# Graph-layer maximum on one core: a shorter chunk part, one-hot columns on GpSimd between gathers, and x theta^T kept in HBM

## The chip, the core and the metric

One NeuronCore of a Trainium2 chip runs the whole kernel. The metric is device time in microseconds (us). Engines: TensorE (PE; PEld is its weight load), VectorE (DVE), ScalarE (ACT), GpSimd (POOL) and SyncE (SP), each with an instruction queue of its own. An indirect DMA (a "gather") fetches one row per partition from HBM by an index in SBUF; GpSimd issues it.

## The reference

`x` is 6250 x 256 float32; 100,000 edges come sorted by `dst`. The weights `theta_w` and `phi_w` are 256 x 256.

```python
x_src, x_dst = x[src], x[dst]
theta_x = (x_dst - x_src) @ theta_w.T + theta_b
phi_x = x_src @ phi_w.T + phi_b
e = relu(theta_x + phi_x)
out = segment_max(e, dst, num_segments=6250)
out = where(isfinite(out), out, 0.0)
return layernorm(x + out)          # eps 1e-5, no affine part
```

For an edge into node n the value is relu(A[n] + B[src]), with A = x theta^T and B = x (phi - theta)^T + both biases. A is the same for all edges of a node, so the kernel takes the maximum of B[src] over the edges of each node and adds A, the relu, x and the normalisation afterwards.

## The kernel before

**Two parts.** B is computed first and written to `b_rows` in HBM. The edges, in the order of `dst`, are then treated in two ways.

*The chunk part* takes the first 128 x `FIRST_STEPS` = 128 x 275 edges, which belong to the first nodes (2154 of them, N1). Each partition holds 275 consecutive edges. A step gathers `b_rows` for one edge of every partition (`gather`, L468); 8 steps are a group (`STEPS`, `gather_group`), so there are 35 groups. `run` (L717) takes a running maximum along a partition's edges on VectorE, which starts anew wherever the node changes (L722, one instruction of 256 columns a step), and writes the group to `maxima_1` in HBM. Segments that cross partitions are mended by `heads_1` (L829), a gather, a maximum and a scatter.

*The node part* has the other 4096 nodes, `TILES` = 32 to a partition (one block of 128 nodes is a tile). It looks up where each node's edges begin (`begin`, from a window of 640 edges by Sign on ACT, L628), gathers each node's source list (`gather_run`, L472, 32 table gathers, read at L475), and then fetches rows of B by matmul instead of by DMA. B's 6250 rows are cut into 17 slots of 375 (`KB` = 3 blocks of 125). For each slot, `choice` (L877, on VectorE, two slots at a time, so nine batches) picks for each node at most one edge whose source lies in it, and `wanted` (L912: transpose on TensorE, a cast `rows` on ACT) writes the row's number to `chosen_rows` in HBM. `slot_part(s, c)` (L939) does a slot for 1024 nodes (four chunks, `CHUNKS`, so 68 parts): it loads the chosen numbers into all partitions (`want`, L945), makes a one-hot matrix `hot` of 128 x 1024 for each of the three blocks, block 0 on VectorE (L949, is_equal) and blocks 1 and 2 on ACT (L951 Abs, L952 Relu), multiplies the slot's rows by it on TensorE in 24 matmuls of 512 columns (L959; each float32 row is split in two `terms` that add up to it), and keeps the maximum in `acc` on VectorE (L970; the first slot is copied by ACT). `slot_terms` (L926) loads a slot's rows and splits them.

Edges that a slot had no place for go into lists (`list_pieces`, L980): `LIST` = 240 steps, 30 groups, which `group_2` (L1044) gathers from `b_rows` and reduces as the chunk part does, into `maxima_2`.

**The order.** The program issues: the sort branch (not taken here: the edges come sorted), table gathers, B, `sources` (L853), nine times `choice`, `wanted` and two chunk groups, the heads of chunks, `list_pieces` with a part between, then the remaining chunk groups with 1.2 parts a group (`PACE`), then the list groups, again with 1.2 parts a group, every third of them with a share of the finishing of the first part's nodes (`rows_of`, L1051, and `normalise`, L1096), then the finish of the node part's 32 tiles. `rows_of` loads x, transposes it, multiplies by theta (L1077), gathers the maxima by node (L468 from `maxima_1` or `maxima_2`, 49 in all), and adds; `normalise` does the layer norm (ACT L1104, L1111). The framework's scheduler may move an instruction on its engine as its dependencies allow.

Gathered groups lie in a ring of 7 tiles (`gathered`, `RING`). Chunk groups 0, 2, 4, 6 and 8 (`X_GROUPS` = 5) gather x itself, before B is there, two of them ahead of the sort branch, and `b_of` (L663) turns the rows into B. B of the whole x goes through `b_of` two tiles at a time: four transposes, an ACT copy `x_t`, four matmuls of 256 columns (L675), and the bias on VectorE (L678).

Of the kernel before, what the change touches and what calls it, by code (L numbers as in the profile page):

```python
# [52 lines left out]
RING = 7  # L53
GENERAL_STEPS = 17
FIRST_STEPS = 275
X_GROUPS = 5
X_BEFORE = 2
TILES = 32
LIST = 240
WINDOW = 640  # L60
# [4 lines left out]
DVE_HOTS = 1  # L65
PACE = 1.2
# [339 lines left out]
def gnn_kernel(ctx: ExitStack, tc: tile.TileContext, x, src, dst, theta_w, theta_b, phi_w, phi_b, out):  # L406
# [4 lines left out]
    Q = N // P  # L411
    LEFT = N - P * Q
    NT = Q + 1
    XQ = 4
# [8 lines left out]
    NB = N // ROWS  # L423
    NS = -(-NB // KB)
# [4 lines left out]
    assert D == 2 * P and LEFT > 0 and LEFT1 > 0 and Q % XQ == 0 and OWN % CW == 0  # L429
    assert (P - 1) * T + 1 < E <= P * T and N < ID_MASK and P * T <= EDGES and E + 8 * P <= EDGES  # L430
    assert N == NB * ROWS and SLOT * NS < ABSENT and KB * P <= SLOT and WINDOW <= 8 * P and P * T1 < E
    assert LIST % STEPS == 0 and TILES <= 32

# [4 lines left out]

    b_rows = dram.tile([N, D], FP, name="b_rows")
# [5 lines left out]

    x_main = x[: P * Q, :].rearrange("(p q) d -> p q d", q=Q)
    b_main = b_rows[: P * Q, :].rearrange("(p q) d -> p q d", q=Q)
    b_block = b_rows.rearrange("(b r) d -> r b d", r=ROWS)


    x_1 = x[: P * Q1, :].rearrange("(p q) d -> p q d", q=Q1)
    x_2 = x[N1:, :].rearrange("(p q) d -> p q d", q=TILES)
    out_1 = out[: P * Q1, :].rearrange("(p q) d -> p q d", q=Q1)
    out_2 = out[N1:, :].rearrange("(p q) d -> p q d", q=TILES)
    maxima_1t = maxima_1[: P * T1, :].rearrange("(p t) d -> p t d", t=T1)
    maxima_2t = maxima_2[: P * LIST, :].rearrange("(p t) d -> p t d", t=LIST)

    def iota(t, step, base, per_partition):
        nc.gpsimd.iota(
            t,  # L460
            pattern=[[step, t.shape[1]]],
            base=base,
            channel_multiplier=per_partition,
            allow_small_or_imprecise_dtypes=True,
        )

    def gather(to, table, offsets):
        nc.gpsimd.indirect_dma_start(  # L468
            out=to, out_offset=None, in_=table, in_offset=bass.IndirectOffsetOnAxis(ap=offsets, axis=0)
        )  # L470

    def gather_run(to, table, offsets):  # L472

        n = to.shape[1]
        nc.gpsimd.indirect_dma_start(  # L475
            out=to,
            out_offset=None,
            in_=flat(table, 0, [[n, EDGES // n], [1, n]]),
            in_offset=bass.IndirectOffsetOnAxis(ap=offsets, axis=1),
        )  # L480
# [15 lines left out]

    for i in of_x[:X_BEFORE]:
        gather_group(i, x)
# [28 lines left out]

    weights = const.tile([P, 2, KC, D], FP, name="weights")
    bias = const.tile([P, 1, D], FP, name="bias")

# [13 lines left out]
    with (  # L544
# [4 lines left out]
        with tc.If(n_unsorted > 0):  # L549
# [4 lines left out]
            for i in of_x[:X_BEFORE]:  # L554
                gather_group(i, x)
# [51 lines left out]
    accs = body.enter_context(tc.tile_pool(name="accs", bufs=1))  # L607
    acc = accs.tile([P, KC, OWN], FP, name="acc")
    index = body.enter_context(tc.tile_pool(name="index", bufs=1))
    dst_w = index.tile([P, WINDOW], I32, name="dst_w")  # L610
    gather_run(dst_w, dst_list, edge0_i)
    for i in of_x[X_BEFORE:]:
        gather_group(i, x)
# [9 lines left out]
    BATCH = 8  # L623
    for j0 in range(0, TILES + 1, BATCH):
        j1 = min(j0 + BATCH, TILES + 1)
        for j in range(j0, j1):
            junk = index.tile([P, WINDOW], BF, name="junk")
            nc.scalar.activation(  # L628
                junk, local, AF.Sign, bias=halves[:, j : j + 1], scale=-1.0, accum_out=sums[:, j : j + 1]
            )  # L630
        nc.vector.tensor_scalar(begin[:, j0:j1], sums[:, j0:j1], 0.5, 0.5 * WINDOW, op0=ALU.mult, op1=ALU.add)
# [8 lines left out]

    with (
        tc.tile_pool(name="prep", bufs=1) as prep,
        tc.tile_pool(name="x_in", bufs=3) as x_in,
        tc.tile_pool(name="b_out", bufs=2) as b_out,
        tc.tile_pool(name="ps_t", bufs=3, space=PSUM) as ps_t,
        tc.tile_pool(name="ps_b", bufs=3, space=PSUM) as ps_b,
    ):
        w_in = prep.tile([P, 2, KC, D], FP, name="w_in")
        for i, w in enumerate((theta_w, phi_w)):
            nc.sync.dma_start(w_in[:, i], w.rearrange("(c p) k -> p c k", p=P))  # L650
        biases = prep.tile([P, 2, D], FP, name="biases")
        for i, b in enumerate((theta_b, phi_b)):
            nc.sync.dma_start(biases[:, i, :], flat(b, 0, [[0, P], [1, D]]))
        nc.vector.tensor_add(bias[:, 0, :], biases[:, 0, :], biases[:, 1, :])
        nc.vector.tensor_sub(w_in[:, 1], w_in[:, 1], w_in[:, 0])
        for i in (1, 0):
            for c in range(KC):
# [3 lines left out]
                nc.vector.tensor_copy(weights[:, i, :, c * P : (c + 1) * P], ps[:, 0])  # L661

        def b_of(to, rows):  # L663

            n = rows.shape[1]
            ps = ps_t.tile([P, 2, KC, P], FP, name="ps_xt")
            for i in range(n):
                for k in range(KC):
                    nc.tensor.transpose(ps[:, i, k, :], rows[:, i, k * P : (k + 1) * P], ident)
            x_t = prep.tile([P, 2, KC, P], FP, name="x_t", bufs=3)  # L670
            nc.scalar.copy(x_t[:, :n], ps[:, :n])  # L671
            ps = ps_b.tile([P, 2, D], FP, name="ps_b")
            for i in range(n):
                for k in range(KC):
                    nc.tensor.matmul(  # L675
# [474 lines left out]
    for j in todo:  # L1150
        node_place(j)
# [74 lines left out]
```

## Time and profile before

| what | value |
|---|---|
| median of 4 runs | 1128.27 us (1126.05 to 1139.71) |
| the profiled execution | 1127.52 us, its span 1125.7 |
| mean granted TensorE clock in the span | 0.783 of full speed |
| DMA over the span | 195.61 MB, 174 GB/s; HBM read 114.27 MB, written 81.38 MB |
| fetch matmuls, L959 | 1600, 432.6 us busy, mean 428 ns |
| chunk gathers, L468 from `b_rows` by `src` | 235, 277.5 us, mean 1181 ns |
| list gathers, L468 from `b_rows` by `list_src` | 240, 233.9 us, mean 974 ns |
| last gathers, L468 from `maxima` | 49, 48.5 us, mean 990 ns |
| running maximum, L722 | 513, 244.2 us, mean 478 ns |
| maximum into `acc`, L970 | 128, 155.5 us, mean 1215 ns |
| one-hot on ACT, L951 and L952 | 132 each, 146.1 and 133.9 us |
| matmuls of B, L675 | 356, 98.5 us |
| matmuls of A at the end, L1077 | 196 (128 for the node part, 68 for the first), 58.1 us |

Times are of one execution by the hardware profiler, engines are busy beside one another, and "idle before" names what ended an engine's idle time. A gather's row is GpSimd's time to issue it; the transfer is done by the DMA engines and lands later. B's last row is written at 139.4 us, the first chunk gather from `b_rows` is issued at 144.3, `choice` ends near 281, `list_pieces` near 338; the list groups run from 534 to 981, and the last write of `maxima` is issued at 1025.

### The profile page before, as it was taken

How to read it: one execution, taken by the hardware profiler on the slowest of the kernel's cores; microseconds unless marked ns; L12 is line 12 of the kernel's file. 1: busy time of each engine (PE TensorE's matmuls, PEld its weight loads, DVE VectorE, ACT ScalarE, POOL GpSimd, SP SyncE). 2: the span in 40 equal slices, each digit the busy share in tenths (PEclk: the TensorE clock that was granted, in tenths of full speed). 3: DMA queues.
4: the chain of work that ended last, by engine and by line, in shares of the span. 5: the costliest groups of instructions: out<-in, count | busy, mean ns of one | idle time of the engine just before them, and what ended most of it. 6: DMA issues, size and time to landing. Idle time of an engine off the chain costs nothing. (4 is left out here: it accounts for less than half of the span.)

```text
span 1125.7 us, 9291 instructions
## 1 busy us (share of the span) xinstructions
PE 644.4 (57%) x2557; PEld 499.0 (44%) x2557; DVE 630.3 (56%) x1309; ACT 429.8 (38%) x680; POOL 638.8 (57%) x622
## 2 busy tenths in 40 slices
PE   0475896485147451287659229447163976795473
PEld 0264784364035340165427128336152755674362
DVE  1221694799979731177487139345253775795264
ACT  0165121564114301166356036336232653650175
POOL 6745377588887777463706736737573657302600
PEclk9888898688658875597859659769585989899696
DMA  6455355477456753375648438546374656645322
GB/s 213 126 160 153 105 181 184 159 247 243 169 165 195 238 173 103 93 233 159 196 183 264 146 102 273 169 138 203 116 224 137 224 186 216 205 180 201 98 99 92
DMA packets 63082, 195.61 MB, mean 174 GB/s; under 512 B 14071, under 2 KB 22795, under 8 KB 53515
## 3 DMA queue, kind: packets, MB, share of 16 engines
q1 hardware_dynamic: 32207, 112.01, 28.3%
q0 software_dynamic: 28272, 75.14, 23.8%
q10 hardware_dynamic: 2540, 7.75, 1.8%
q8 instruction: 23, 0.38, 0.1%
q14 instruction: 40, 0.33, 0.1%
HBM read 114.27 MB, written 81.38 MB: 174 GB/s over the span
## 5 line engine op out<-in xcount | busy, mean ns | idle before, releaser
L959 PE MATMUL ps_f<-hot,terms 128*128 128x512 f32 x1600 | 432.6, 428 | 290.7 <-issue 107.2
L959 PEld LDWEIGHTS ps_f<-hot,terms 128*128 128x128 f32 x1600 | 327.9, 208 | 384.4 <-issue 217.9
L468 POOL DMA_INDIRECT g<-b_rows,src x235 | 277.5, 1181 | 109.3 <-issue 70.2
L468 POOL DMA_INDIRECT g<-b_rows,list_src x240 | 233.9, 974 | 160.8 <-issue 68.9
L970 DVE TENSOR_TENSOR acc<-acc,ps_f 128x1024 f32<-128x1024 f32 x128 | 155.5, 1215 | 249.5 <-remote 216.6
L951 ACT ACTIVATE hot<-want,minus_row 128x1024 fp32r<-128x1024 f16 x132 | 146.1, 1145 | 332.2 <-remote 218.0
L722 DVE SCALAR_TENSOR_TENSOR g<-g,caps 128x256 f32<-128x256 f32 x513 | 244.2, 478 | 21.5 <-issue 15.3
L952 ACT ACTIVATE hot<-hot 128x1024 fp32r<-128x1024 f32 x132 | 133.9, 1049 | 0.4
L675 PE MATMUL ps_b<-weights,x_t 128*128 128x256 f32 x356 | 98.5, 437 | 47.1 <-ACT x_t L671 32.8
L468 POOL DMA_INDIRECT g<-maxima,place x49 | 48.5, 990 | 105.5 <-issue 62.9
L675 PEld LDWEIGHTS ps_b<-weights,x_t 128*128 128x128 f32 x356 | 75.7, 219 | 66.4 <-ACT x_t L671 37.6
L1077 PE MATMUL ps_e<-weights,x_t 128*128 128x256 f32 x128 | 37.6, 442 | 34.2 <-ACT x_t L1073 18.2
L671 ACT COPY x_t<-ps_xt 128x512 f32<-128x512 f32 (+1 forms) x45 | 24.9, 578 | 76.7 <-remote 24.7
L949 DVE TENSOR_SCALAR hot<-want,row_id 128x1024 fp32r<-128x1024 f16 x68 | 51.0, 750 | 1.4 <-ACT hot L952 1.4
L475 POOL DMA_INDIRECT table_i<-src_list,begin_i x32 | 30.3, 946 | 33.4 <-DVE begin_i L632 24.5
L468 POOL DMA_INDIRECT g<-in_x_dram,src x40 | 39.1, 977 | 16.0 <-issue 11.3
L678 DVE TENSOR_TENSOR b_sb<-ps_b,bias 128x512 f32<-128x512 f32 (+1 forms) x25 | 16.6, 678 | 52.1 <-remote 23.0
L1077 PEld LDWEIGHTS ps_e<-weights,x_t 128*128 128x128 f32 x128 | 26.1, 215 | 42.2 <-ACT x_t L1073 22.5
L628 ACT ACTIVATE junk<-local,halves 128x640 bf16<-128x640 f32 x33 | 27.4, 829 | 31.5 <-DVE b_sb L678 17.8
L1077 PE MATMUL ps<-weights,x_t 128*128 128x256 f32 x68 | 20.5, 452 | 32.6 <-issue 18.4
L1104 ACT ACTIVATE squares<-g,r 128x256 bf16<-128x256 f32 x49 | 24.3, 498 | 33.9 <-DVE g L722 25.2
L1087 DVE TENSOR_TENSOR g<-g,ps_e 128x512 f32<-128x512 f32 (+1 forms) x17 | 11.1, 655 | 44.2 <-PE ps_e L1086 20.1
(194 smaller groups left out, 498.7 us busy)
## 6 DMA issues: line engine op xcount, KB each, us to landing
maxima<-g SPq DMA_DIRECT2D x64, 1024.0 KB
want<-chosen_rows SPq DMA_DIRECT2D x68, 256.0 KB
x_q<-in_x_dram SPq DMA_DIRECT2D x12, 512.0 KB
b_rows<-b_sb ACTq DMA_DIRECT2D x12, 512.0 KB
raw<-b_rows SPq DMA_DIRECT2D x16, 336.0 KB
g<-in_x_dram SPq DMA_DIRECT2D x5, 1024.0 KB
out_dram<-g SPq DMA_DIRECT2D x5, 1024.0 KB
g<-b_rows,list_src POOLq DMA_INDIRECT x240
```

The source lines that it names most:

```text
L468: nc.gpsimd.indirect_dma_start(out=to, out_offset=None, in_=table, in_offset=bass.IndirectOffsetOnAxis(ap=offsets, axis=0))
L475: nc.gpsimd.indirect_dma_start(out=to, out_offset=None, in_=flat(table, 0, [[n, EDGES // n], [1, n]]), in_offset=bass.IndirectOffsetOnAxis ...
L628: nc.scalar.activation(junk, local, AF.Sign, bias=halves[:, j : j + 1], scale=-1.0, accum_out=sums[:, j : j + 1])
L671: nc.scalar.copy(x_t[:, :n], ps[:, :n])
L675: nc.tensor.matmul(ps[:, i, :], x_t[:, i, k, :], weights[:, 1, k, :], start=(k == 0), stop=(k == KC - 1))
L722: nc.vector.scalar_tensor_tensor(g[:, k, :], last[part], caps[:, t : t + 1], g[:, k, :], op0=ALU.min, op1=ALU.max)
L949: nc.vector.tensor_scalar(hot[:, b, :], want, row_id[:, b : b + 1], None, op0=ALU.is_equal)
L951: nc.scalar.activation(hot[:, b, :], want, AF.Abs, bias=minus_row[:, b : b + 1], scale=1.0)
L952: nc.scalar.activation(hot[:, b, :], hot[:, b, :].bitcast(FP), AF.Relu, bias=1.0, scale=-1.0)
L959: nc.tensor.matmul(ps[:, w : w + 512], terms[:, part, b, h * P : (h + 1) * P], hot[:, b, w : w + 512], start=(i == 0), stop=(i == n - 1),)
L970: nc.vector.tensor_tensor(to, to, ps, op=ALU.max)
L1077: nc.tensor.matmul(a[:, i, :], x_t[:, 2 * i + c, :], weights[:, 0, c, :], start=(c == 0), stop=(c == KC - 1))
```

## The change

- **Sizes.** The chunk part has 146 steps a partition (19 groups, the last of two steps) instead of 275, the node part 40 nodes (5120 nodes; five chunks of 1024, so 85 parts), the lists 288 steps (36 groups), the window 800 edges.
- **One-hot of block 0 on GpSimd.** `slot_part` is split. `start_part` loads `want`, makes block 0's one-hot on GpSimd and blocks 1 and 2 on ACT; `finish_parts` issues the matmuls and the maxima. `gather_steps` calls `start_part` ahead of every fourth gather while its group has parts left: one part in a chunk group, two in a list group; `finish_parts` stands behind the group's `run`.
- **GpSimd's order is fixed.** `in_turn` gives each of these GpSimd instructions an order dependency on the one before, so that they run as the program is written. A gather that is neither followed by a one-hot nor has one to come in its group is followed by an iota of 144 columns into a scratch tile `pause`.
- **A = x theta^T beside B.** A pair of tiles is multiplied by both weights in matmuls of 512 columns; ACT copies A out and it is written to `a_rows` in HBM. `rows_of` loads it from there in place of transposes, copies and matmuls of its own.
- **Slots by consecutive rows.** A slot is 375 consecutive rows of B, row p*3+b in block b of partition p, so that a slot's load takes three whole rows a partition; `sources` computes the row's place accordingly.
- **Rings and small moves.** Three groups of x (one ahead of the branch) instead of five; a ring of 4 tiles for the chunk part, and one of 7 for the lists and the finish, which lies where the tables were. Of ten begin positions three are counted by Sign on ACT and seven by is_le with a sum on VectorE. `choice` is followed by one chunk group, not two. `heads_1` gathers after the fourth list group and scatters after the sixth. The finish takes shares of eight tiles, four a PSUM tile.

```diff
-RING = 7
...
-FIRST_STEPS = 275
-X_GROUPS = 5
-X_BEFORE = 2
-TILES = 32
-LIST = 240
-WINDOW = 640
+RING = 4
+RING_2 = 7
+FIRST_STEPS = 146
+X_GROUPS = 3
+TILES = 40
+LIST = 288
+WINDOW = 800
...
-DVE_HOTS = 1
-PACE = 1.2
+PAUSE = 144
...
+    pause = const.tile([P, PAUSE], FP, name="pause")
...
+    def in_turn(one):
+        if latest[0] is not None:
+            after = mybir.DependencyInfo(mybir.DependencyClass.NoSync, mybir.DependencyReason.DATA)
+            tc.add_manual_dep(one.ins, latest[0], after, reason="GpSimd's order")
+        latest[0] = one.ins.name
+    def indirect(out, in_, in_offset=None, out_offset=None):
+        in_turn(nc.gpsimd.indirect_dma_start(out=out, out_offset=out_offset, in_=in_, in_offset=in_offset))
+    def gather(to, table, offsets, alone=True):
+        indirect(to, table, bass.IndirectOffsetOnAxis(ap=offsets, axis=0))
+        if alone:
+            in_turn(iota(pause, 1, 0, 0))
...
+    def gather_steps(to, sources, n, starts):
+        for k in range(n):
+            more = False
+            if starts and (k + 1) % (STEPS // 2) == 0:
+                more = start_part()
+                starts = starts - 1 if more else 0
+            gather(to[:, k, :], b_rows, sources[:, k : k + 1], alone=not (more or starts))
...
+                x_t = x_transposed(x_q[:, i : i + w, :])
+                ps = ps_b.tile([P, 2, 2, D], FP, name="ps_b")
+                for h in range(w):
+                    for k in range(KC):
+                        nc.tensor.matmul(
+                            ps[:, h], x_t[:, h, k, :], weights[:, k], start=(k == 0), stop=(k == KC - 1)
+                        )
+                add_bias(b_sb[:, i : i + w, :], ps[:, :w, 0, :])
+                nc.scalar.copy(a_sb[:, i : i + w, :], ps[:, :w, 1, :])
+            nc.scalar.dma_start(node_rows(b_rows, *share), present(b_sb, *share))
+            nc.scalar.dma_start(node_rows(a_rows, *share), present(a_sb, *share))
...
-    def group_1(i):
-        if i not in of_x:
-            gather_group(i, b_rows)
+    def group_1(i, starts):
         t0, n = groups[i]
-        run(1, ring_tiles[i], n, caps_1, t0, maxima_1t)
+        if i in of_x:
+            g = ring_tiles[i]
+            for _ in range(starts):
+                start_part()
+        else:
+            g = gathered.tile([P, STEPS, D], FP, name="g")
+            gather_steps(g, src_1[:, t0 : t0 + n], n, starts)
+        run(1, g, n, caps_1, t0, maxima_1t)
+        finish_parts()
...
-        nc.gpsimd.indirect_dma_start(out=maxima_1, out_offset=at_heads, in_=heads, in_offset=None)
+        in_turn(iota(pause, 1, 0, 0))
+        yield
+        indirect(maxima_1, heads, out_offset=at_heads)
...
+        left = min(SLOT_ROWS, N - s * SLOT_ROWS)
+        whole = left // KB
+        even = whole // 16 * 16
+        for a, b in ((0, even), (even, whole)):
+            if b > a:
+                nc.sync.dma_start(
+                    raw[a:b], flat(b_rows, (s * SLOT_ROWS + a * KB) * D, [[KB * D, b - a], [D, KB], [1, D]])
+                )
...
+        nc.scalar.copy(terms[:, 0], raw)
+        nc.vector.tensor_tensor(terms[:, 1], raw, terms[:, 0].bitcast(FP), op=ALU.subtract)
...
+    parts = [(s, c) for s in range(NS) for c in range(CHUNKS)]
+    started = []
+    def start_part():
+        if not parts:
+            return False
+        s, c = parts.pop(0)
         if c == 0:
             slot_terms(s)
-        blocks = min(KB, NB - s * KB)
-        terms = terms_of[s]
         want = slots.tile([P, CW], HF, name="want")
         nc.sync.dma_start(want, flat(chosen_rows, s * OWN + c * CW, [[0, P], [1, CW]]))
...
-            if b < DVE_HOTS:
-                nc.vector.tensor_scalar(hot[:, b, :], want, row_id[:, b : b + 1], None, op0=ALU.is_equal)
-            else:
-                nc.scalar.activation(hot[:, b, :], want, AF.Abs, bias=minus_row[:, b : b + 1], scale=1.0)
-                nc.scalar.activation(hot[:, b, :], hot[:, b, :].bitcast(FP), AF.Relu, bias=1.0, scale=-1.0)
...
+        in_turn(nc.gpsimd.tensor_scalar(hot[:, 0, :], want, row_id[:, 0:1], None, op0=ALU.is_equal))
+        for b in range(1, KB):
+            nc.scalar.activation(hot[:, b, :], want, AF.Abs, bias=minus_row[:, b : b + 1], scale=1.0)
+            nc.scalar.activation(hot[:, b, :], hot[:, b, :].bitcast(FP), AF.Relu, bias=1.0, scale=-1.0)
+        started.append((s, c, hot))
+        return True
+    def finish_parts():
+        while started:
+            s, c, hot = started.pop(0)
+            terms = terms_of[s]
+            for h in range(KC):
+                ps = ps_fetch.tile([P, CW], FP, name="ps_f")
+                n = KB * PARTS
+                for i in range(n):
+                    b, part = divmod(i, PARTS)
+                    for w in range(0, CW, 512):
+                        nc.tensor.matmul(
...
+                to = acc[:, h, c * CW : (c + 1) * CW]
+                if s == 0:
...
-    def group_2(t0):
-        g = gathered.tile([P, STEPS, D], FP, name="g")
-        for k in range(STEPS):
-            gather(g[:, k, :], b_rows, list_src[:, t0 + k : t0 + k + 1])
+    def group_2(t0, starts):
+        g = ring_2.tile([P, STEPS, D], FP, name="g")
+        gather_steps(g, list_src[:, t0 : t0 + STEPS], STEPS, starts)
         run(2, g, STEPS, caps_2, t0, maxima_2t)
...
+        finish_parts()
...
+        nc.sync.dma_start(present(x_f, *share), node_rows(x, *share))
+        nc.sync.dma_start(present(a, *share), node_rows(a_rows, *share))
+        m = ring_2.tile([P, STEPS, D], FP, name="g")
...
+        for k in range(n):
+            gather(m[:, k, :], maxima, places[:, j0 + k : j0 + k + 1])
...
-            a = ps_tile().rearrange("p (i d) -> p i d", i=2)
-            for i in range(w):
-                for c in range(KC):
-                    nc.tensor.matmul(
-                        a[:, i, :], x_t[:, 2 * i + c, :], weights[:, 0, c, :], start=(c == 0), stop=(c == KC - 1)
-                    )
-            two = m[:, k : k + w, :]
+        for k in range(0, n, 4):
+            w = min(4, n - k)
+            some = m[:, k : k + w, :]
...
+            nc.vector.tensor_tensor(some, some, a[:, k : k + w, :], op=ALU.add)
...
+    todo = list(range(NT1))
+    def next_group_1():
+        if groups_1:
+            group_1(groups_1.pop(0), 1)
+        if todo:
+            node_place(todo.pop(0))
     sources()
     for s0 in range(0, NS, BATCH_S):
         choice(s0)
         wanted(s0)
-        for _ in range(2):
-            group_1(groups_1.pop(0))
-        if s0 == 0:
-            fetch_parts(1)
+        next_group_1()
...
-            group_1(groups_1.pop(0))
-        fetch_parts(1)
-    pace = 0.0
-    while groups_1:
-        group_1(groups_1.pop(0))
-        if todo:
-            node_place(todo.pop(0))
-        pace += PACE
-        while pace >= 1.0:
-            fetch_parts(1)
-            pace -= 1.0
-    for j in todo:
-        node_place(j)
+            next_group_1()
+    tables.close()
+    ring_2 = body.enter_context(tc.tile_pool(name="ring_2", bufs=RING_2, side="right"))
+    while groups_1 or todo:
+        next_group_1()
     places_1()
...
-    while lists:
-        group_2(lists.pop(0))
-        pace += PACE
-        while pace >= 1.0:
-            fetch_parts(1)
-            pace -= 1.0
-        if len(lists) % 3 == 0 and (shares or waiting):
+    heads = heads_1(carried)
+    for i in range(LIST // STEPS):
+        group_2(i * STEPS, 2)
+        if i in (3, 5):
+            next(heads, None)
...
-    fetch_parts(len(parts))
+    assert not early_shares
+    while start_part():
+        finish_parts()
```

## The prediction

> **What bounds the kernel now.** I read the page's totals, then the waits, then GpSimd and TensorE in order of time, then busy time by stage. Totals and waits first (who waited <- for whom: us, times, longest):
>
> ```profile
> span 1125.7 us, 9291 instructions
> PE 644.4 (57%) x2557; PEld 499.0 (44%) x2557; DVE 630.3 (56%) x1309; ACT 429.8 (38%) x680; POOL 638.8 (57%) x622
> ...
> ACT hot L951 <- remote: 218.0, 13, 45.7
> PEld ps_f L959 <- issue: 217.9, 52, 18.9
> DVE acc L970 <- remote: 216.6, 20, 30.0
> ```
>
> No engine is full. Three engines each lose some 217 us to waits that name no local work, and they lose them together. TensorE in such a stretch, then GpSimd in the same one (start, duration, instruction, idle before):
>
> ```profile
> 415.67 0.39 PE L959 MATMUL ps_f<-hot,terms 128*128 128x512 f32 x1 [1.51 <-issue]
> 418.48 0.58 PE L959 MATMUL ps_f<-hot,terms 128*128 128x512 f32 x1 [2.42 <-issue]
> 421.27 0.59 PE L959 MATMUL ps_f<-hot,terms 128*128 128x512 f32 x1 [2.21 <-issue]
> ...
> 480.90 5.83 PE L959 MATMUL ps_f<-hot,terms 128*128 128x512 f32 x24
> ```
>
> ```profile
> 416.11 0.95 POOL L468 DMA_INDIRECT g<-b_rows,src  x1 [0.30 <-issue]
> 417.36 0.95 POOL L468 DMA_INDIRECT g<-b_rows,src  x1 [0.30 <-issue]
> 418.61 0.95 POOL L468 DMA_INDIRECT g<-b_rows,src  x1 [0.30 <-issue]
> ```
>
> TensorE crawls at one matmul in 2 to 3 us where 24 take 5.83 us at 480.9, while GpSimd issues gathers at an exact 1.25 us (0.95 + 0.30 of idle). This holds wherever I looked: every unbroken run of 24 or more gathers at 1.25 to 1.29 us (394-467, 534-564, 598-660, 690-741, 756-807) brings all other engines to a crawl some 10 to 20 us in, and they recover by some 7 us after GpSimd pauses. Runs of 8 (676, 914, 971) bring none, and in 222-395, where VectorE's work stretches the pitch to 1.4 us and more, VectorE is never idle for 5 us. Stages (us, busy PE, PEld, DVE, ACT, POOL, clock, DMA share):
>
> ```profile
> 222.00:395.00 173.00, 88.56 (x319) 67.67 (x319) 156.09 (x303) 64.77 (x70) 141.41 (x103) 0.77 0.64 211
> 394.00:478.00 84.00, 26.88 (x68) 17.25 (x69) 15.43 (x38) 8.46 (x13) 55.83 (x58) 0.58 0.42 121
> 600.00:1025.00 425.00, 260.93 (x1038) 204.68 (x1037) 234.65 (x419) 179.85 (x221) 227.20 (x232) 0.79 0.57 181
> ```
>
> In 394-478 only GpSimd works. Then its ring of gather tiles is full of rows that nobody reduced, it stops, and the others catch up: turns instead of overlap. In 600-1025, 232 gathers at 1.25 us are 290 us of 425. The prices below start from these groups (busy us, mean ns of one, idle before):
>
> ```profile
> L949 DVE TENSOR_SCALAR hot<-want,row_id 128x1024 fp32r<-128x1024 f16 x68 | 51.0, 750 | 1.4 <-ACT hot L952 1.4
> L859 POOL IOTA rank<- 128x1152 f32 x1 | 1.3, 1299 | 0.0
> L991 POOL IOTA rank<- 128x1152 f32 x1 | 1.1, 1092 | 12.8 <-DVE work L866 12.8
> masks.py:199 POOL TENSOR_SCALAR_AFFINE_SELECT ident<-ident 128x128 f32<-128x128 f32 x1 | 0.3, 299 | 0.0
> ```
>
> **What the change moves.** Chunk gathers fall from 275 to 146 steps, list gathers rise from 240 to 288, table gathers from 32 to 40, last gathers from 49 to 49 (9 + 40): GpSimd issues some 525 indirect DMAs for some 597. Slot parts rise from 68 to 85 (17 x 5), so 2,040 fetch matmuls for 1,600. GpSimd also makes 85 one-hots. Elsewhere a short iota into `pause` follows each gather.
>
> *One-hot on GpSimd.* The trace has none. Bounds from its rows: an iota of 1152 columns takes 1.09 to 1.30 us, so 1024 take about 1.15; the affine select of 128 takes 0.30 against 0.13 for a one-column iota, 1.3 ns a column, so up to 1.55. I take 1.35. It reads SBUF, beside VectorE's reads; no row shows that pair, so I allow up to double in the rivals. VectorE loses 68 x 0.75 = 51 us of it, off the path.
>
> The Trainium skill speaks against this move (GPSIMD Engine Reference, Engine selection): elementwise work belongs on VectorE, GpSimd being about half as fast on two inputs and near line rate on one. By the first, twice VectorE's 0.75 us row, an estimate of 1.5 us would add 13 us to the sum below; by the second, 0.75 would take 51 off it. Its SBUF — State Buffer (Who interferes with whom) adds that a VectorE instruction with two SBUF inputs contends with a GpSimd instruction that reads SBUF; no row here shows that pair.
>
> *The pause.* An iota starts at the end of a gather with no gap (59.13 behind the gather at 58.18), and three 128-column iotas cost 0.62. So a pause costs 0 if it fits the 0.30 us gap and 0.22 if the gap comes after it: pitch 1.25 or 1.47. I take 0.1 in the sum and believe in the larger for the crawl.
>
> *Preparation, until the first chunk gather (144.3 now).* Eight x gathers instead of sixteen ahead of the branch bring everything behind it forward by about 9 us. Forty table gathers, from about 44, end near 103 (now 123). Then VectorE: `sources` is 11.3 us of rows x 1.25 = 14, two more passes make 17; a `choice` is 6.6 us (6.4 of rows x 1.25, less overlap) x 8.5 = 56. In the built order all of it stands among the 19 evictions of B (0.62 each, 12) that are left by then: 106 + 85 = 191. TensorE has for a pair of tiles 4 matmuls of 512 columns, twice the 0.46 us that one of 256 takes in rows of 16 records in 3.72 us, and four transposes, 4.2 us in all: 19 pairs are 80 us at full clock, 94 at the 0.85 granted here, so 200. Copying A out of PSUM (25 x 0.58 us on ACT) and its write lie beside this. The first one-hot is now ahead of the first gather on GpSimd, in fixed order. It waits for `want`, that for `chosen_rows`, that for ACT's cast, which stands behind nearly all copies of the x groups (12 pairs x 2.33 us of TensorE). Every gather waits behind it. The two transfers take about 5 us each (the last b_rows write was issued at 139.4, its first reader began at 144.3). Bounds: 195 if TensorE keeps full clock and runs ahead, 235 if all is serial. I take **215**, 71 later than now.
>
> *Chunk stage.* 122 gathers x 1.25 = 153; 18 one-hots x 1.35 = 24; two iotas 3; 50 pauses x 0.1 = 5; VectorE's list building lengthens gathers now (27 in 281-338 took 57 us for 34, so 23), x 1.25 = 28. Sum **213**, bounds 195 to 235. VectorE holds some 150 us here and hides.
>
> *List stage.* A group is 8 gathers x 1.25 = 10, two one-hots 2.7, and 0.5 because gathers lengthen beside VectorE (974 ns mean in this stage, 1035 in 675-703, for 947 clean): 13.2 us. TensorE has 48 matmuls, 11.7 us at 24 in 5.83; VectorE 8 x 0.40 + 4 x 1.14 + 0.4 = 8.2; ACT 4 x 2.2 + 0.3 = 9.1. So GpSimd sets it and TensorE is close behind; a part's one-hot tile comes round after two parts, so TensorE cannot lag. 34 groups x 13.2 = 449, two without one-hots 21, 9 last gathers and the heads' two 16: **486**. Bounds 12.2 (TensorE) to 14.5 a group: 452 to 530. The 24.1 us wait for `heads` goes, since it now stands four groups later.
>
> *End.* Last landing, run and write, 2 + 3 + 5 = **10**. Forty gathers at 1.25 to 1.47, 54; last landing 2, VectorE 8, root 2, squares 8 x 0.6, scaling 8 x 0.5, write 5: 84, less 4 of overlap, **80** (72 to 95). Now 101 us lie behind the last maxima write at 1025; x theta^T read from HBM takes 128 matmul records (37.6 us) and their copies out.
>
> Sum 215 + 213 + 486 + 10 + 80 = 1004; with the 1.8 us that lie around the span (1127.52 for 1125.7), **1006**. The profiled run is 0.8 us under the median of 1128.27.
>
> **Rivals.** *1, slower: the crawl stays.* If pauses vanish in the gap and a one-hot per four gathers is no break, then a part costs what it does in 600-1025, 43 parts in 425 us, 9.9 each: 67 parts are 663 for 449, and preparation and end lose some 20: about 1,240. For it: a pause may leave the pitch at 1.25. Against: 4 gathers and a one-hot have a mean pitch of 1.59, where 1.4 showed no gap. It decides if crawl needs less than a mean pitch of about 1.3; slower than now begins at 17.1 us a group. *2, faster:* TensorE, not GpSimd, sets the list stage (12.2 a group, 452), preparation ends at 195, chunk 195, end 72: 926. For it: the 0.30 us may hide beneath a one-hot. *3, no gain:* one-hots contend and take 2.7 us (85 x 1.35 more, 115), preparation at its worst bound adds 20: about 1,140 less what TensorE hides, so 1,115 to 1,140. For it: VectorE reads two SBUF operands in every step of a run. *4, the relief is not from pitch* but from VectorE's own work; then 1 holds in part.
>
> **Numbers.** Forecast case 0.65, its own range 950 to 1070; rival 2 0.17; rival 1 (with 4) 0.11; rival 3 0.07. A difference under 1% cannot be told from none: runs here spread over 1126 to 1140. The range reaches from rival 2 to the upper bounds of the forecast: 915 to 1095. Faster 0.84, same 0.04, slower 0.12.
>
> **What would show it.** Waits `<- remote` and `<- issue` of TensorE, VectorE and ACT fall from some 217 us each to under 60; no single fetch matmul every 2 us; GpSimd's one-hot row at 1.15 to 1.55 us; a list group every 13.2 us; the first b_rows gather at 195 to 235 behind a one-hot that waits. Wrong, if the one-hot row passes 2 us, if GpSimd waits for `hot` or `want` in the list stage, or if gathers at 1.25 us still stand beside an idle VectorE.

## The result, and the profile after

The changed kernel takes 1176.3 us (median of 20 runs, 1173.95 to 1182.24) beside 1127.67 for the kernel before: a ratio of 1.0499, 95% interval 1.0473 to 1.0526. The prediction said 1006, range 915 to 1095. It is slower by 5% where a gain of 11% was forecast. Some executions of a kernel are 2 to 4% longer than others of the same kernel: ratios are of the faster ones, medians of all, and the range of the runs stands where there is no ratio.

The totals of the changed kernel, and below them the chief waits (who waited <- for whom: us, times, longest):

```profile
span 1173.8 us, 9473 instructions
...
PE 723.6 (62%) x2607; PEld 528.8 (45%) x2607; DVE 731.4 (62%) x1172; ACT 476.8 (41%) x666; POOL 847.3 (72%) x820
```

```profile
DVE g L761 <- DMA g<-b_rows,list_src: 181.6, 120, 5.7
ACT hot L1007 <- PE ps_f L1022: 178.5, 28, 16.5
PEld ps_f L1022 <- POOL hot L1005: 141.4, 28, 16.2
POOL hot L1005 <- DMA want<-chosen_rows: 131.1, 3, 129.3
PE ps_f L1022 <- POOL hot L1005: 120.2, 20, 15.4
POOL g L483 <- issue: 116.8, 456, 7.9
PEld ps_f L1022 <- issue: 109.0, 41, 5.9
...
PE ps_f L1022 <- issue: 7.6, 2, 5.5
```

The waits `<- remote` of VectorE and ACT, some 217 us each before, are gone. TensorE's weight load still shows 109.0 us `<- issue` for 217.9, where under 60 was forecast. Its matmuls, which no row of the prediction shows, had this wait too in the kernel before:

```profile
PE ps_f L959 <- issue: 107.2, 40, 16.8
```

That is 7.6 now. VectorE now waits for gathered rows, ACT for TensorE, TensorE for GpSimd's one-hot. These waits lead to GpSimd, whose busy time rose from 638.8 to 847.3 us. The crawl has been traded for a queue. GpSimd in the list stage, and one line of the chunk stage (start, duration, instruction, idle before):

```profile
289.75 2.87 POOL L1005 TENSOR_SCALAR hot<-want,row_id 128x1024 fp32r<-128x1024 f16 x1
...
707.61 2.87 POOL L1005 TENSOR_SCALAR hot<-want,row_id 128x1024 fp32r<-128x1024 f16 x1
710.65 1.03 POOL L483 DMA_INDIRECT g<-b_rows,list_src  x1 [0.17 <-issue]
711.99 0.95 POOL L483 DMA_INDIRECT g<-b_rows,list_src  x1 [0.30 <-issue]
713.24 0.95 POOL L483 DMA_INDIRECT g<-b_rows,list_src  x1 [0.30 <-issue]
714.49 0.96 POOL L483 DMA_INDIRECT g<-b_rows,list_src  x1 [0.30 <-issue]
715.47 2.88 POOL L1005 TENSOR_SCALAR hot<-want,row_id 128x1024 fp32r<-128x1024 f16 x1
```

From one-hot to one-hot are 7.86 us with nothing but the 0.17 to 0.30 us that stand ahead of each gather, so a list group is 15.7 us. The one-hot takes 2.87 us, not 1.35; over 2 us was the prediction's own sign of being wrong. Its group, with two others (busy us, mean ns of one, idle before):

```profile
L761 DVE SCALAR_TENSOR_TENSOR g<-g,caps 128x256 f32<-128x256 f32 x432 | 284.1, 659 | 242.2 <-DMA g<-b_rows,list_src 181.6
L1005 POOL TENSOR_SCALAR hot<-want,row_id 128x1024 fp32r<-128x1024 f16 x85 | 245.1, 2884 | 137.4 <-DMA want<-chosen_rows 131.1
L483 POOL DMA_INDIRECT g<-b_rows,list_src x288 | 285.2, 990 | 77.0 <-issue 72.2
```

By stage, from the start of each in GpSimd's timeline, for the two profiled executions:

| stage | before | forecast | after |
|---|---|---|---|
| preparation, to the first one-hot (before: first chunk gather) | 144.3 | 215 | 232.7 |
| chunk stage, to the first list gather | 389.9 | 213 | 246.4 |
| list stage, to the end of the last list gather | 447 | 486 | 577.3 |
| behind it | 144.6 | 90 | 117.4 |
| span | 1125.7 | 1004 | 1173.8 |

Against before, the shorter chunk part gave back 144 us and the end 27, while preparation took 88 more and the longer list stage 130.

### The profile page after: what moved, and what is told of

Read it like the earlier page. It is cut to its first block, busy times and chain, and to the rows that moved or that the text cites. A ratio compares the mean times of both kernels' runs of the same rounds, so it can differ in the third digit from the quotient of the medians.

```text
span 1173.8 us, 9473 instructions
## 1 busy us (share of the span) xinstructions
PE 723.6 (62%) x2607; PEld 528.8 (45%) x2607; DVE 731.4 (62%) x1172; ACT 476.8 (41%) x666; POOL 847.3 (72%) x820
## 5 line engine op out<-in xcount | busy, mean ns | idle before, releaser
L1022 PE MATMUL ps_f<-hot,terms 128*128 128x512 f32 x2040 | 558.1, 437 | 239.3 <-POOL hot L1005 120.2
L1022 PEld LDWEIGHTS ps_f<-hot,terms 128*128 128x128 f32 x2040 | 430.1, 214 | 364.5 <-POOL hot L1005 141.4
L761 DVE SCALAR_TENSOR_TENSOR g<-g,caps 128x256 f32<-128x256 f32 x432 | 284.1, 659 | 242.2 <-DMA g<-b_rows,list_src 181.6
L1005 POOL TENSOR_SCALAR hot<-want,row_id 128x1024 fp32r<-128x1024 f16 x85 | 245.1, 2884 | 137.4 <-DMA want<-chosen_rows 131.1
L483 POOL DMA_INDIRECT g<-b_rows,list_src x288 | 285.2, 990 | 77.0 <-issue 72.2
L1007 ACT ACTIVATE hot<-want,minus_row 128x1024 fp32r<-128x1024 f16 x170 | 186.1, 1142 | 273.4 <-PE ps_f L1022 178.5
L483 POOL DMA_INDIRECT g<-b_rows,src x122 | 140.9, 1155 | 27.6 <-issue 25.8
L720 PE MATMUL ps_b<-weights,x_t 128*128 128x512 f32 x196 | 96.4, 648 | 54.5 <-ACT x_t L700 42.7
L720 PEld LDWEIGHTS ps_b<-weights,x_t 128*128 128x128 f32 x196 | 39.7, 209 | 103.5 <-ACT x_t L700 56.1
L724 ACT COPY a_sb<-ps_b 128x512 f32<-128x512 f32 (+1 forms) x25 | 14.4, 578 | 112.3 <-DVE b_sb L704 97.5
L463 POOL IOTA pause<- 128x144 f32 x186 | 51.5, 277 | 1.5
```

What stands on the lines that cost most here:

```text
L463: return nc.gpsimd.iota(t, pattern=[[step, t.shape[1]]], base=base, channel_multiplier=per_partition, allow_small_or_imprecise_dtypes=True,)
L483: in_turn(nc.gpsimd.indirect_dma_start(out=out, out_offset=out_offset, in_=in_, in_offset=in_offset))
L720: nc.tensor.matmul(ps[:, h], x_t[:, h, k, :], weights[:, k], start=(k == 0), stop=(k == KC - 1))
L761: nc.vector.scalar_tensor_tensor(g[:, k, :], last[part], caps[:, t : t + 1], g[:, k, :], op0=ALU.min, op1=ALU.max)
L1005: in_turn(nc.gpsimd.tensor_scalar(hot[:, 0, :], want, row_id[:, 0:1], None, op0=ALU.is_equal))
L1007: nc.scalar.activation(hot[:, b, :], want, AF.Abs, bias=minus_row[:, b : b + 1], scale=1.0)
```

## Experiments

Two accounts stood against each other. The first: the breaks between gathers did relieve the other engines, as forecast, but each was bought with 2.87 us of the engine that issues the gathers. The second: the gain was never there, or the one-hot is long only because it contends.

**The one-hot back on VectorE, with and without breaks.** Three kernels from the changed one have this edit:

```diff
-        in_turn(nc.gpsimd.tensor_scalar(hot[:, 0, :], want, row_id[:, 0:1], None, op0=ALU.is_equal))
+        nc.vector.tensor_scalar(hot[:, 0, :], want, row_id[:, 0:1], None, op0=ALU.is_equal)
```

e1 is that alone. e2 has a pause behind every gather besides, e3 one pause where the one-hot stood:

```diff
-            gather(to[:, k, :], b_rows, sources[:, k : k + 1], alone=not (more or starts))
+            gather(to[:, k, :], b_rows, sources[:, k : k + 1], alone=True)
```

```diff
+        in_turn(iota(pause, 1, 0, 0))
```

> The changed kernel with block 0's one-hot back on VectorE and nothing in its place on GpSimd, so list gathers stand in unbroken runs at 1.25 us. Theory (long unbroken runs make the other engines crawl; the one-hot on GpSimd broke the runs but cost 2.87 us each of GpSimd's own time): the crawl comes back, waits <- remote and <- issue of TensorE, VectorE and ACT rise again above 100 us each, a list group stays above 15 us, total 1130 to 1250. Rival (the runs are harmless here, only GpSimd's 85 x 2.87 = 245 us were lost): no crawl, a list group 12 to 12.5 us set by TensorE, total 970 to 1030.

> As e1, with the short iota behind every gather, pitch 1.41 us. Theory: no crawl, since no pitch of 1.4 showed one; a list group is 8 x 1.41 = 11.3 us of GpSimd and 11.7 to 12.2 of TensorE, so 12 to 12.5 us for 15.8; chunk stage 146 less 24 steps at 1.41 plus lengthening, about 205; preparation the same or 5 us shorter since no gather waits for a one-hot; total 960 to 1030. Rival (crawl comes from something else than the pitch, and only the one-hot's 2.9 us relieved it): as e1, 1130 or more.

> As e1, with one short iota on GpSimd where each one-hot stood: a break of 0.16 us for every four gathers in the list stage, mean pitch 1.29. If any break relieves: as e2, 960 to 1030, a list group 12 to 12.5 us. If the crawl depends on the mean pitch (none at 1.4, full at 1.25 to 1.29): crawl as in e1, 1130 to 1250. Theory leans to the second.

Measured: e1 1095.79 us (ratio to before 0.9674, 0.959 to 0.9759), e2 982.7 (0.8695, 0.8642 to 0.8748), e3 1078.78 (0.9541, 0.947 to 0.9611). The waits of e1, and TensorE in order of time:

```profile
PEld ps_f L1022 <- issue: 173.1, 48, 24.6
ACT hot L1007 <- remote: 165.2, 11, 56.3
DVE acc L1033 <- remote: 148.1, 17, 26.3
```

```profile
594.05 3.07 PE L1022 MATMUL ps_f<-hot,terms 128*128 128x512 f32 x11 [1.79 <-DVE acc L1033]
597.69 0.40 PE L1022 MATMUL ps_f<-hot,terms 128*128 128x512 f32 x1 [0.57 <-issue]
...
671.69 4.89 PE L1022 MATMUL ps_f<-hot,terms 128*128 128x512 f32 x10 [12.19 <-issue]
678.10 0.39 PE L1022 MATMUL ps_f<-hot,terms 128*128 128x512 f32 x1 [1.52 <-issue]
```

With a pitch of 1.25 us again (from the start of one gather to the start of the next) the waits without a local cause are back, and so are single matmuls with gaps `<-issue`. e1's time, though, is 34 us below its expected range: its list groups alternate between 10 us and 20 to 42 (mean 14.8), less than the 16.2 of the changed kernel. It also issues its first chunk gather at 195.3 for 235.7, since none waits behind a one-hot. So GpSimd's one-hots cost more than the crawl that they remove. In e2 the waits `<- remote` of VectorE and ACT are under 3 us each (the longest row is shown), and a list group takes 12.8 us on average:

```profile
PEld ps_f L1022 <- issue: 155.5, 28, 23.5
...
ACT hot L1007 <- remote: 2.6, 1, 2.6
```

TensorE's weight load still shows 155.5 us `<- issue`, though e2 does not crawl: that row alone does not tell a crawl, and the prediction's "under 60" for it was a wrong sign. The matmuls' row does: 111.0 in e1, and no such row in e2. The breaks are worth 1095.79 - 982.7 = 113 us here, and they cost no more than 0.16 us a gather. e1 and e2 have the same order on GpSimd, so the pauses alone make this difference. e3, with one short break for four gathers, crawls (187 us of VectorE's wait `<- remote`, in an execution of 1096.42 us), as the theory had it, though in less time than it expected.

**One part alone in the kernel before.** Order and pauses, and nothing else:

```diff
...
     def gather(to, table, offsets):
-        nc.gpsimd.indirect_dma_start(
-            out=to, out_offset=None, in_=table, in_offset=bass.IndirectOffsetOnAxis(ap=offsets, axis=0)
-        )
+        in_turn(
+            nc.gpsimd.indirect_dma_start(
+                out=to, out_offset=None, in_=table, in_offset=bass.IndirectOffsetOnAxis(ap=offsets, axis=0)
+            )
+        )
+        in_turn(iota(pause, 1, 0, 0))
```

> The kernel before with one part of the change alone: GpSimd's gathers in program order with a 144-column iota behind each. Theory: the crawl goes without any other part: waits <- remote of VectorE and ACT and <- issue of TensorE fall from some 217 us to under 60 each; the list stage, 447 us now, falls to 240 x 1.41 = 338 plus breaks, about 350 to 380; total 1000 to 1070. Rival (pauses only lengthen GpSimd's sequence): 524 x 0.16 = 84 us more, about 1200.

1020.13 us, ratio 0.9029 (0.8964 to 0.9094). A pause of 0.28 us behind each gather, which does nothing, makes the kernel before 10% faster. VectorE's wait `<- remote` for TensorE's results fell from 216.6 to 19.7 us, and that of TensorE's matmuls `<- issue` from 107.2 to 14.4 (its weight load keeps 169.0):

```profile
DVE acc L985 <- remote: 19.7, 7, 5.1
PE ps_f L974 <- issue: 14.4, 6, 5.3
```

The list stage takes 400 us, though, not 350 to 380: three of its groups, between which the 17 gathers of the first part's shares stand, take 23 to 32 us, and I had left those gathers out.

And the one-hot of the kernel before on GpSimd, alone:

```diff
-                nc.vector.tensor_scalar(hot[:, b, :], want, row_id[:, b : b + 1], None, op0=ALU.is_equal)
+                nc.gpsimd.tensor_scalar(hot[:, b, :], want, row_id[:, b : b + 1], None, op0=ALU.is_equal)
```

> The kernel before with block 0's one-hot on GpSimd and nothing else. Theory: 68 x 2.87 = 195 us more of GpSimd's time; 43 parts in the list stage break the gathers about every 5.6; the crawl goes as in the changed kernel, the list stage is 240 x 1.25 + 43 x 2.95 = 427 for 447, so what is gained on the crawl is paid to the one-hot: total 1080 to 1180, no clear gain. Rival (the one-hot is cheap in this arrangement or the order on GpSimd matters): below 1060.

1179.62 us (1174.79 to 1185.31), beside 1138.09 (1104.78 to 1149.44) for the kernel before on the same chip: every run is longer than all of before. TensorE's matmuls waited 349.2 us for the one-hot, which again takes 2.9 (busy us, mean ns of one, idle before):

```profile
L949 POOL TENSOR_SCALAR hot<-want,row_id 128x1024 fp32r<-128x1024 f16 x68 | 197.8, 2911 | 32.3 <-PE ps_f L959 25.8 <-DMA want<-chosen_rows 4.8
```

VectorE's wait `<- remote` fell from 216.6 to 12.0 us, though its wait `<- issue` ahead of the same instruction rose from 18.6 to 81.4, so the relief is not whole. So this one move, by itself, shows both sides of the change: relief and a dearer queue.

**What the one-hot costs and why.** Ten forms on scratch data in the stretch where GpSimd has nothing else to do (`f_in`, `f_out` f32, `h_in`, `h_out` f16, `b_out` bf16, `r_out` fp32r), twice each:

```diff
...
+    in_turn(nc.gpsimd.tensor_scalar(r_out, h_in, one, None, op0=ALU.is_equal))
+    in_turn(nc.gpsimd.tensor_scalar(r_out[:, : CW // 2], h_in[:, : CW // 2], one, None, op0=ALU.is_equal))
...
+    in_turn(nc.gpsimd.tensor_scalar(f_out, f_in, one, None, op0=ALU.is_equal))
...
+    in_turn(nc.gpsimd.tensor_copy(f_out, f_in))
+    in_turn(iota(f_out, 1, 0, 0))
```

> The changed kernel plus, in the stretch where GpSimd waits for the first want (104 to 232 us), ten forms of an elementwise instruction on scratch data, twice each: the one-hot as it is (f16 in, fp32r out, 1024 columns), half as wide, f32 out, a constant in place of the per-partition operand, f32 in and out, f16 out, bf16 out, a subtraction f32, a copy f32, an iota. What is computed is the same. Theory (2.87 us is the instruction's own length): the one-hot takes 2.85 to 2.9 here too, half the columns 1.43; a copy or iota of 1024 about 1.15, which is where the prediction's 1.35 came from. If the f16 input is what costs, f32 in takes 1.2 to 1.5; if the per-partition operand costs, the constant form does. If contention with other work made it long, it takes 1.2 to 1.5 in some of these places. Total unchanged within 1%.

```profile
107.16 2.85 POOL L676 TENSOR_SCALAR acc<-acc,row_id 128x1024 fp32r<-128x1024 f16 x1
...
132.90 1.06 POOL L684 COPY acc<-acc 128x1024 f32<-128x1024 f32 x1
134.03 0.99 POOL L463 IOTA acc<- 128x1024 f32 x1
135.12 4.38 POOL L676 TENSOR_SCALAR acc<-acc,row_id 128x1024 fp32r<-128x1024 f16 x1
139.59 1.78 POOL L677 TENSOR_SCALAR acc<-acc,row_id 128x512 fp32r<-128x512 f16 x1
...
144.54 2.77 POOL L679 TENSOR_SCALAR acc<-acc 128x1024 fp32r<-128x1024 f16 x1
147.41 3.20 POOL L680 TENSOR_SCALAR acc<-acc,row_id 128x1024 f32<-128x1024 f32 x1
150.59 2.84 POOL L681 TENSOR_SCALAR acc<-acc,row_id 128x1024 f16<-128x1024 f16 x1
```

A copy of 1024 columns takes 1.06 and 1.66 us and an iota 0.99, but no compare or subtract of that width falls below 2.77, whatever its types and whether its operand is a constant (L679) or not. So neither the f16 input nor the operand is dear: it is the class of instruction (all of them are `tensor_scalar`; no other arithmetic was tried). This was not a quiet place: VectorE's work of `sources` and `choice` lay beside it, and the same form took 2.85 and 4.38, the half width 2.10 and 1.78. The half width is therefore not settled here. The time rose to 1197.94, outside "within 1%": the first one-hot moved from 232.7 to 252.1, and VectorE's own instructions ahead of it grew longer beside the probe (the first pass of `sources` over 1440 columns took 2.10 us for 0.91).

Then half the suspected cost taken away:

```diff
-        in_turn(nc.gpsimd.tensor_scalar(hot[:, 0, :], want, row_id[:, 0:1], None, op0=ALU.is_equal))
+        half = CW // 2
+        in_turn(nc.gpsimd.tensor_scalar(hot[:, 0, :half], want[:, :half], row_id[:, 0:1], None, op0=ALU.is_equal))
+        nc.vector.tensor_scalar(hot[:, 0, half:], want[:, half:], row_id[:, 0:1], None, op0=ALU.is_equal)
```

> The changed kernel with half of block 0's one-hot (512 columns) on GpSimd and the other half on VectorE. Theory (the one-hot lies whole on GpSimd's serial path at 2.8 ns a column): 1.43 us each, a list group 15.8 - 2 x 1.43 = 12.9 us, just above TensorE's 12.2, no crawl; the time falls by 85 x 1.43 = 122 us, to 1045 to 1080, and that is the case the prediction's sum of 1006 was made for, but for preparation and end. Rival (the time was lost elsewhere, in the wait for want or in VectorE's instructions held up beside the one-hot): falls by less than 60.

1100.68 us (ratio 0.9683, 0.9627 to 0.974): 76 less than the changed kernel (92 by the ratios to the kernel before), between the two expectations and above the first's range. The half takes 1.57 us at least and 1.715 on average, not 1.43, so some 0.3 us of an instruction do not go with its width. 85 x (2.884 - 1.715) = 99 us of GpSimd's time are gone, and 76 to 92 of them show.

Finally the forecast's own price in the place of the one-hot: an iota of 1024 columns, the one-hot being VectorE's.

```diff
...
-        in_turn(nc.gpsimd.tensor_scalar(hot[:, 0, :], want, row_id[:, 0:1], None, op0=ALU.is_equal))
+        nc.vector.tensor_scalar(hot[:, 0, :], want, row_id[:, 0:1], None, op0=ALU.is_equal)
+        in_turn(iota(wide, 1, 0, 0))
```

> The changed kernel with block 0's one-hot on VectorE and, at its place on GpSimd, an iota of 1024 columns (0.99 us alone) into a scratch tile. Four gathers at 1.25 and a break of 1.0 + 0.16: mean pitch 1.54. If the mean pitch over some gathers decides on the crawl, none here: a list group 8 x 1.25 + 2 x 1.2 = 12.4 us, total 990 to 1030. If every single pitch must be above 1.34: crawl, 1070 to 1110. I lean to the first, since the changed kernel has four gathers at 1.25 between one-hots and no crawl.

```profile
701.20 1.00 POOL L463 IOTA wide<- 128x1024 f32 x1
702.36 1.22 POOL L484 DMA_INDIRECT g<-b_rows,list_src  x1 [0.16 <-issue]
703.88 0.95 POOL L484 DMA_INDIRECT g<-b_rows,list_src  x1 [0.30 <-ACT hot L1009]
705.14 0.95 POOL L484 DMA_INDIRECT g<-b_rows,list_src  x1 [0.30 <-issue]
706.39 1.19 POOL L484 DMA_INDIRECT g<-b_rows,list_src  x1 [0.30 <-issue]
707.58 1.01 POOL L463 IOTA wide<- 128x1024 f32 x1
```

992.87 us (0.8739, 0.8688 to 0.8789), with a list group of 12.9 us on average. Four gathers and a 1.0 us break do hold off the crawl. This is nearly the case that the forecast described. That it lies 13 us from 1006 is partly chance: no chunk gather waits for a one-hot here, so the first comes at 196.4 for 215, and the end takes 112 for 90.

**How long a break must be.** e2 with 1 and with 64 columns in `pause`:

```diff
-PAUSE = 144
+PAUSE = 1
```

> e2 with a pause of 1 column in place of 144. It takes about 0.13 us, so with the gap of 0.16 behind it the pitch is about 1.25 us, as without one. If the pitch decides on the crawl: as e1, 1080 to 1110. If an instruction between two gathers is enough: as e2 or some us less, 965 to 985. I lean to the pitch.

> e2 with a pause of 64 columns: about 0.18 us, pitch about 1.31 to 1.33. If the crawl sets in below about 1.3: as e2 less 288 x 0.08 where GpSimd sets the pace, 965 to 985. If it needs 1.4: between e2 and e1, 990 to 1090.

1122.78 us (1120.52 to 1143.3) and 1099.51 (1078.39 to 1112.39, the longest profiled). GpSimd in e8, then in e2:

```profile
601.01 0.95 POOL L483 DMA_INDIRECT g<-b_rows,list_src  x1 [0.16 <-issue]
601.97 0.21 POOL L463 IOTA pause<- 128x64 f32 x1
602.33 0.96 POOL L483 DMA_INDIRECT g<-b_rows,list_src  x1 [0.15 <-issue]
```

```profile
602.28 0.95 POOL L483 DMA_INDIRECT g<-b_rows,list_src  x1 [0.16 <-issue]
603.24 0.28 POOL L463 IOTA pause<- 128x144 f32 x1
603.67 1.19 POOL L483 DMA_INDIRECT g<-b_rows,list_src  x1 [0.16 <-issue]
```

The pitch is 1.32 us in e8 and 1.39 or more in e2 (1.26 to 1.27 in e7). An instruction between the gathers is no help by itself: e7 has one behind each and waits `<- remote` 201.6 us on VectorE, e8 168.7. Both my boundary for e8 (1.3) and e7's upper bound were too hopeful; e8's runs lie on both sides of its upper bound of 1090.

**Two more parts.** e11 is e2 with VectorE's first instruction of `sources` (`one`) held behind the last eviction of B (`last_b`), by this edge; e12 is e2 with the old sizes (275, 32, 240, 640).

```diff
...
+        tc.add_manual_dep(one.ins, last_b.ins.name, behind, reason="VectorE's order")
```

> e2 with one order edge more: VectorE's first instruction of sources stands behind its last eviction of B. In the changed kernel it stands ahead of many and waits 27 us for the table gathers while TensorE waits for the evictions. Theory: B is in HBM some 25 to 30 us earlier, the first chunk gather at 170 to 178 for 198, total 955 to 975 for 983. Rival (the choice batches, now later, hold up the first parts as much): 980 to 990.

> e2 with the sizes of before: 275 steps, 32 tiles, lists of 240, a window of 640. GpSimd: 235 + 24 + 240 + 49 gathers for 122 + 288 + 49, so 65 more at 1.41 = 92 us, and TensorE 68 parts for 85. If GpSimd's gathers set the time: about 1040 to 1080. If TensorE does: 930 to 980.

e11 takes 997.4 us for e2's 982.7. The first chunk gather came at 179.4 for 198.5, as expected, but the work that VectorE did while B was made now lies in the chunk stage: it is busy 229 of the 250 us from 175 to 425 (192 in e2). So the place of that instruction did hold up preparation, by 19 us, but the total did not gain: the chunk stage took 245 us for 211, and the expected 955 to 975 was wrong. e12 takes 1061.03, inside the range for "GpSimd's gathers set the time", so the new sizes are worth 78 us once the crawl is gone (73 by the ratios). Its expectation miscounts: by its own terms 89 gathers are added and not 65, and the kernel has 81 more (251 + 240 + 49 for 122 + 288 + 49), 114 us at 1.41.

## Why the prediction was wrong

*The step that failed* is the one-hot on GpSimd: "I take 1.35", bounded by 1.15 to 1.55. It measured 2.884 on average, with a floor of 2.85. The bounds came from an iota, which reads no data, and an affine select of 128 columns, the nearest rows of the trace, but neither compares a whole tile with an operand. The term is 85 x (2.884 - 1.35) = 130 us too small, beside the 170 by which the sum was short: 18 one-hots in the chunk stage, 28 us of its 33 too many, and 67 in the list stage, 103, where the stage is 91 over.

VectorE's row for the same one-hot was 750 ns, so GpSimd takes 3.8 times as long. The Trainium skill (GPSIMD Engine Reference, Engine selection), weighed against this move, has elementwise work on VectorE, which the runs bear out; its figures, about twice as slow on two inputs and near line rate on one, do not fit, since this instruction has one full-width input.

*Rival 3* named the right price (2.7 us) for the wrong reason and at the wrong total. The one-hot at 368.02, with no VectorE instruction beside it, takes 2.87 us, the one at 715.47, with VectorE busy all along, 2.88; 82 of the 85 take 2.85 to 2.89. And "less what TensorE hides" hid little, since GpSimd sets the pace. 1006 + 130 alone is 1136.

*The mechanism was right.* The crawl goes when GpSimd's mean pitch is long enough (changed kernel, e2, e4, e10, and in the main e6) and comes back when it is not (e1, e3, e7, e8). Rival 1 had the point from which it decides at "a mean pitch of about 1.3"; the runs put it between 1.32 (e8) and 1.39 (e2), the pitches that the lines above show. e10 shows that single intervals of 1.25 us do no harm where a break of 1.16 us follows every four gathers; whether it is the mean pitch or the length of an unbroken run that decides, no run separates.

*The pause* was put between 0 and 0.22, and I took 0.1: it is 0.14 to 0.16 (pitch 1.39 to 1.41 for 1.25, with a gap of 0.16 left behind the iota).

*Preparation* came to 232.7, near my bound for "all is serial". VectorE stood 27 us in front of the table gathers, TensorE's last matmul for the whole x ended at 193, the twelve pairs of the x groups took until 225, and ACT's first cast `rows` behind them came at 225.9; then two transfers. I had overlapped what is serial. (e11 bears this out in part: it moves VectorE's instruction and brings the first chunk gather 19 us forward.)

*The end* came to 117.4 for 90. The first of the forty last gathers is 8 us behind the last list gather, and they take 78 us, not 54: GpSimd waited 9.9, 6.1 and 1.9 us for VectorE before three of them. A share now needs three of the ring's seven tiles (x, A, maxima). This is read from the trace; no run here tried a larger ring. The prediction's own terms for this stretch add up to 80 before the overlap is taken off, not to 84, and the upper bounds of all stages to 1107, not 1095; neither slip changes the outcome.

The whole as a sum over kernels, from runs on different chips in part: the kernel before 1128; pauses alone -112 (e4); the rest of the change at old sizes, with pauses and VectorE's one-hot, +41 (e12 over e4; the first chunk gather is at 185.5 for 141.5); the new sizes -78 (e2 over e12); the one-hot on GpSimd in place of pauses +194 (changed kernel over e2; 34 of them are preparation, since the first gather stands behind the first one-hot). That makes 1173 beside 1176, but each step is a difference of two neighbours, so that the sum had to close and proves nothing by itself.

The best version is e2, the change without its GpSimd one-hot and with a pause behind every gather: 982.7 us, 13% under the kernel before.

## What to carry to other kernels

Where a stage is bound by one engine's sequence of issues, price what is put between them on that engine by a row of the same class of instruction, or measure one before moving 85. If all that is wanted is a break, buy the shortest one that works: 0.16 us a gather (e2) removed the crawl as 0.72 us a gather (the one-hots) did. And an engine's idle time that names no local work can come from another engine's rate of issue, which a do-nothing instruction in its queue tests in one run.

## What the runs showed of the hardware

*The rate of indirect DMAs slows other engines.* Gathers of 128 rows at a mean pitch of 1.25 to 1.32 us bring VectorE and ACT to waits `<- remote` of over 140 us each in e1, e3, e7 and e8, and TensorE's matmuls to 68 to 111 us `<- issue`; at some 1.4 (e2), or with 1.16 us more for every four (e10), each of these is under 3 us (the kernel before with pauses, e4, keeps 14 to 20 of them on VectorE and TensorE). What carries it was not found: DMA was busy only 42% in such a stretch of the kernel before (394 to 478 us).

*GpSimd's arithmetic holds up VectorE's two-operand instructions.* The running maximum takes 0.484 us where it does not meet a one-hot, and 0.870 on average for the 196 that do. One of them, in VectorE's timeline, beside the one-hot at 289.75 above:

```profile
287.76 0.48 DVE L761 SCALAR_TENSOR_TENSOR g<-g,caps 128x256 f32<-128x256 f32 x1
289.04 2.12 DVE L761 SCALAR_TENSOR_TENSOR g<-g,caps 128x256 f32<-128x256 f32 x1 [0.80 <-DMA g<-b_rows,src]
```

It ends at 291.16, 1.41 us into the one-hot, half of its 2.87. Of the 64 that take over 0.7 us, 61 end 1.40 to 1.43 us into a one-hot; of the 75 that start later in one than that, 74 take their usual 0.48. The maximum into `acc`, whose other operand lies in PSUM, is untouched: 1.214 us clear of one-hots, 1.215 beside them. Beside the `tensor_scalar` forms of e5, a VectorE pass with a single tensor operand grew too (the 2.10 us for 0.91), so two operands are not a condition for every instruction. The Trainium skill (SBUF — State Buffer, Who interferes with whom) says that two SBUF inputs contend with a GpSimd instruction that reads SBUF, which agrees; it also says that the loser waits for the whole instruction, for the modes in which VectorE takes both ports, and here the wait ended at the half. Whether these 76 us (196 x 0.386) of VectorE cost any of the time is not shown; VectorE stood idle 181.6 us for gathered list rows.
